# Moving two copies of the scan layer's ScalarE order, and leaving one background place empty

## The chip, the cores and the metric

The kernel runs on one core of one Trainium2 chip. The metric is the device time of one execution in microseconds. Before the change it is 13172.89 us, the median of 3 runs (13163.58 to 13174.3).

## The reference

The program is a chain of four layers on `x` of 8 x 64 x 64 x 64, all in fp32. Only layer 0 is touched. It normalises the 64 channels, projects them to two halves of 128, convolves one half (3 x 3, depthwise, SiLU), and runs a selective scan over the 4096 pixels in four directions `k`, with 16 states `N` for each of 128 channels:

```
def step(h, inp):
    u_t, dt_t, B_t, C_t = inp
    h = h * jnp.exp(dt_t[..., None] * A) + dt_t[..., None] * B_t[:, :, None, :] * u_t[..., None]
    return (h, jnp.einsum('bkcn,bkn->bkc', h, C_t))
```

The four directions' results are summed, normalised, multiplied by SiLU of the other half (the gate `z`), projected back to 64 channels and added to `x`. A second block of the layer and three attention or normalisation layers follow; nothing of them changes here.

## The kernel before

`scan_layer` works image by image (8), and in each image through 16 **steps**: directions in the order 0, 2, 1, 3, and in each four chunks of 1024 pixels. A step has 16 **turns** `n`, counted from 0, one for each state. The order of all instructions is written out by hand (`manual_schedule`), and each engine runs its own in that order.

In turn `n` SP issues two loads of rows broadcast to 128 partitions, `bt` of three turns ahead (four buffers) and `ct` of one turn ahead (five buffers). ACT computes `decay` (L575), `a = exp(dt * A)`, two turns ahead. `unit` makes `bdu = bt * du` on DVE (L594, in PSUM), scans (L598, result `h`, three buffers), lets ACT copy the last column to `state` (L602), and lets POOL multiply `ct` by `h` (L607). PE adds that product into `yps` by a matmul with the identity (`sum_up`, L636), two turns late (`LAG`). In turns 3 and 8 (`BY_POOL`) the product with the step input is POOL's, in place in `bt` (L583), made two turns ahead; the scan then reads `bt`, and POOL's multiplication of the turn before is put off until after it.

At the ends of a step:

- the step input `dus = dt * u` is made on POOL for the next step (`step_input`, L548, after turn 11), and ACT copies it into PSUM as `du` (`place_input`, L554) in turn 15, when the last `bdu` has read the old one. There is one `du`.
- the sum of turn 15 is made by PE in turn 1 of the next step. `yps` has one buffer. `empty` (L616) lets ACT copy it to `y`, called at the head of `sum_up`, so in turn 2, behind that turn's `decay` and `state`; then PE opens the new `yps` with the old `y` or the skip term (L631) and adds turn 0.
- in the directions 1 and 3 ACT first gathers the chunk's columns into `ut` (L534).

Everything else is a queue of **background** items (`Background`). `before` takes one item at the head of a turn and issues its matmuls; `after`, at a turn's end, uses the item taken a turn earlier, mostly on ACT. Items of the next step (its projections, L487 to L525) go ahead of the others. Behind them wait, for the finished image, a normalisation and eight output projections (`xo`, L454, with a POOL multiplication of `z` and `y` each, L441); and for the next image, loads, a normalisation, eight projections into `pad`, eight gates (`z`, L390), and eight convolutions in four parts (`u`, L414). Gates and convolutions use SiLU, which costs ACT a table load, and another one for the next exponential. Ahead of step 15 of an image what is left in the queue is emptied at once.

Of the kernel before, what the change touches and what calls it, by code (L numbers as in the profile page):

```python
# [24 lines left out]
N = 16  # L25
# [139 lines left out]
class Background:  # L165
# [14 lines left out]
    def later(self, do):  # L180
        self.late.append(do)

    def before(self):
        self.now = None
        if self.queue:
            make, use = self.queue.popleft()
            self.now = (use, make() if make else None)

# [14 lines left out]
def scan_layer(cm, x_in, w, xh):  # L203

    tc, nc = cm.tc, cm.nc
    with ExitStack() as ctx:
# [51 lines left out]
        skip = cm.tile([DI, 1], "skip")  # L258
# [7 lines left out]
        bg = Background()  # L266
# [202 lines left out]
        def ordered(t, k, c):  # L469

            if k % 2 == 0:
                return t[:, bass.ts(c, CH)].rearrange("p (a b) -> p a b", b=S)
            q = CH // S
            return t.rearrange("p (h w) -> p w h", w=S)[:, c * q : (c + 1) * q, :]
# [70 lines left out]
        def step_input(ctl):  # L545

            ctl["dus"] = work.tile([DI, CH], F32, name="dus", tag="dus", bufs=1)
            nc.gpsimd.tensor_tensor(ctl["dus"], ctl["dt"], ctl["ut"]["u"], ALU.mult)  # L548

        def place_input(ctl):  # L550


            ctl["du"] = psy.tile([DI, CH], F32, name="du", tag="du")
            nc.scalar.copy(ctl["du"], ctl["dus"])  # L554
# [11 lines left out]
        def load(ctl, n, t):  # L566

            bcr = ctl["bc"].rearrange("(t n) l -> t n l", t=2)
            name = "bt" if t == 0 else "ct"
            ctl[name, n] = bcp.tile([DI, CH], F32, name=name, tag=name, bufs=4 + t)  # L570
            nc.sync.dma_start(ctl[name, n], bcr[t, n].unsqueeze(0).broadcast_to([DI, CH]))

        def decay(ctl, n):
            ctl["a", n] = work.tile([DI, CH], F32, name="a", tag="a", bufs=3)
            nc.scalar.activation(  # L575
                ctl["a", n], ctl["dt"], AF.Exp, scale=amat[:, ctl["k"], n : n + 1]
            )
# [7 lines left out]
        def unit(ctl, n, nxt):  # L585

            k, state = ctl["k"], ctl["state"]
            a, bt, ct = ctl.pop(("a", n)), ctl.pop(("bt", n)), ctl.pop(("ct", n))
            flip = slice(None, None, -1 if k >= 2 else 1)
            last = 0 if k >= 2 else CH - 1  # L590
            z = bt
            if n not in BY_POOL:
                z = psy.tile([DI, CH], F32, name="bdu", tag="bdu")
                nc.vector.tensor_tensor(z, bt, ctl["du"], ALU.mult)  # L594
            if n == N - 1 and nxt:
                place_input(nxt)
            h = work.tile([DI, CH], F32, name="h", tag="h", bufs=3)
            nc.vector.tensor_tensor_scan(  # L598
                h[:, flip], a[:, flip], z[:, flip],
                0.0 if state is None else state[:, n : n + 1], ALU.mult, ALU.add,  # L600
            )
            nc.scalar.copy(ctl["new"][:, n : n + 1], h[:, last : last + 1])  # L602
            ready.append((ctl, n, ct, h))
            if n + 1 not in BY_POOL:
                while ready:
                    ctl, n, ct, h = ready.pop()
                    nc.gpsimd.tensor_tensor(ct, ct, h, ALU.mult)  # L607
                    pending.append((ctl, n, ct))
# [3 lines left out]
        def empty():  # L612

            if full:
                ctl = full.pop()
                nc.scalar.copy(  # L616
                    ordered(ctl["y"], ctl["k"], ctl["c"]),
                    ctl["ps"].rearrange("p (a b) -> p a b", b=S),
                )

        def sum_up():


            empty()
            ctl, n, ct = pending.popleft()
            if n == 0:
                ctl["ps"] = psy.tile([DI, CH], F32, name="yps", tag="yps")
                wt, src = (skipd, ctl["u"]) if ctl["k"] == 0 else (cm.ident, ctl["y"])
                so, half = ordered(src, ctl["k"], ctl["c"]), BK // S
                for i in range(CH // BK):  # L630
                    nc.tensor.matmul(  # L631
                        ctl["ps"][:, bass.ts(i, BK)].rearrange("p (a b) -> p a b", b=S),
                        wt, so[:, i * half : (i + 1) * half, :], start=True, stop=False,
                    )
            for i in range(CH // BK):
                nc.tensor.matmul(  # L636
                    ctl["ps"][:, bass.ts(i, BK)], cm.ident, ct[:, bass.ts(i, BK)],
                    start=False, stop=(n == N - 1),
                )
            if n == N - 1:  # L640
                full.append(ctl)
# [7 lines left out]
        def prepare(b, s):  # L649

            if b not in images:
                return None
            u, zd, y = images[b]
            k, c, i = steps[s]
            dt, bc, ut, items, soft3 = project(u, k, c)
            if b == 0 and s < NCH:
                items = later.pop(s, []) + items
            bg.add(items, first=True)
            new = work.tile([DI, N], F32, name="state", tag="state", bufs=3)
            return dict(  # L660
                k=k, c=c, u=u, y=y, dt=dt, bc=bc, ut=ut, soft3=soft3, new=new, state=None,
                first=(i == 0),
            )
# [5 lines left out]
        def start(b):  # L669
            u, zd, items, gates, convs = before(b)  # L670
            y = io.tile([DI, L], F32, name="y", tag="y")
            images[b] = (u, zd, y)
            bg.add(items)
            if b == 0:
                for s in range(1, NCH):
                    later[s] = convs[2 * s] + convs[2 * s + 1]
                bg.add(convs[0] + convs[1])
                later[NCH] = gates
            else:
                bg.add(gates)  # L680
                for conv in convs:
                    bg.add(conv)


        with tc.manual_schedule():
            start(0)
            bg.drain()
            ctl = prepare(0, 0)
            bg.drain()
            ctl["soft3"]()  # L690
            for n in range(3):
                load(ctl, n, 0)
            load(ctl, 0, 1)
            for n in range(2):
                decay(ctl, n)
            step_input(ctl)
            place_input(ctl)
            for b in range(NB):
                for s in range(len(steps)):
                    if s + 1 < len(steps):  # L700
                        nxt = prepare(b, s + 1)
                    else:
                        while bg.queue:
                            bg.before()
                            bg.after()
                        nxt = prepare(b + 1, 0)

                    def ahead(do, m, *args):
                        if m < N:
                            do(ctl, m, *args)  # L710
                        elif nxt:
                            do(nxt, m - N, *args)

                    for n in range(N):
                        bg.before()
                        ahead(load, n + 3, 0)
                        ahead(load, n + 1, 1)
                        ahead(decay, n + 2)
                        ahead(product, n + 2)
                        unit(ctl, n, nxt)  # L720
                        if len(pending) + len(ready) > LAG:
                            sum_up()
                        bg.after()

                        if n == (13 if b == 0 and s < NCH else 8) and nxt:
                            nxt["soft3"]()
                        if n == (13 if b == 0 and s < NCH else 11) and nxt:
                            step_input(nxt)

                        if s == 0 and n == LAG + 2 and b > 0:  # L730
                            bg.add(after(b - 1, images[b - 1][2], images.pop(b - 1)[1]))
                        if s == (1 if b else NCH) and n == 0 and b + 1 < NB:
                            bg.add(later.pop(NCH, []))
                            start(b + 1)
                    if nxt:
                        if not nxt["first"]:
                            nxt["state"] = ctl["new"]
                    ctl = nxt
            while pending:
                sum_up()  # L740
            empty()
            bg.add(after(NB - 1, images[NB - 1][2], images[NB - 1][1]))
            bg.drain()
# [1137 lines left out]
```

## Time and profile before

| | us |
|---|---|
| median of 3 runs | 13172.89 |
| profiled execution, time | 13181.03 |
| profiled execution, span | 13179.2 |
| DVE busy | 10982.4 (83% of the span) |
| PE busy | 11127.1 (84%) |
| ACT busy | 7731.6 (59%) |
| POOL busy | 6776.3 (51%) |
| in the scans' stretch, 121 to 7724 us: DVE busy | 7163.89 of 7603 |
| POOL, PE, ACT busy there | 6050.95, 6061.36, 4793.03 |

The page is one execution taken by the hardware profiler. A group's row gives line, engine, operation, result and inputs, shape and count; then busy time and mean nanoseconds of one; then the engine's idle time just before the group's instructions and what ended it. In a timeline the columns are start, length, engine, line, operation, and in brackets the idle time before. A wait for several semaphores is put down to the one that came last.

### The profile page before, as it was taken

The page shows a single profiled execution, that of the slowest core. Times are in us where ns is not written, and L with a number is a line of the kernel's source. Part 1 is how long each engine was busy: PE and PEld are TensorE (multiplying, and loading weights), DVE is VectorE, ACT ScalarE, POOL GpSimd, SP SyncE. Part 2 cuts the span into 40 slices and gives each one's busy share as a digit, 9 for nine tenths or more (in the row PEclk, how much of TensorE's full clock was granted, in tenths as well). Part 3 has the DMA queues.
Part 4 walks back from the last instruction along what each step waited for, and adds up shares of the span by engine and source line. Part 5 has one row for each costly group of instructions (what it writes and reads, how often), then busy time and mean ns, then how long its engine had stood idle before and what let it go on. Part 6 is the DMA issues. An engine that isn't in the chain of part 4 may idle for free. (4 is left out here: it accounts for less than half of the span.)

```text
span 13179.2 us, 115966 instructions
## 1 busy us (share of the span) xinstructions
PE 11127.1 (84%) x36395; PEld 4134.4 (31%) x36395; DVE 10982.4 (83%) x7626; ACT 7731.6 (59%) x10048; POOL 6776.3 (51%) x3126
## 2 busy tenths in 40 slices
PE   8787887788888878877877779999997778999999
PEld 2232232232232232322322223323324554333332
DVE  6999999999999999999999958686686786666666
ACT  5675666665666766665765536455464674544544
POOL 5778878778778778778778840000002772000000
PEclk9898999898999999999998879999998788999999
DMA  5888888888888888888888840000001010000000
GB/s 196 289 281 291 302 290 294 293 286 301 292 285 306 288 291 300 290 285 303 288 287 299 289 158 9 23 13 17 17 6 63 29 37 25 5 17 17 5 11 6
DMA packets 684840, 2333.69 MB, mean 177 GB/s; under 512 B 96784, under 2 KB 97456, under 8 KB 681648
## 3 DMA queue, kind: packets, MB, share of 16 engines
q1 hardware_dynamic: 684208, 2326.13, 51.1%
q8 instruction: 290, 4.75, 0.1%
q14 instruction: 342, 2.80, 0.1%
HBM read 2240.69 MB, written 76.28 MB: 176 GB/s over the span
## 5 line engine op out<-in xcount | busy, mean ns | idle before, releaser
L607 POOL TENSOR_TENSOR ct<-ct,h 128x1024 f32<-128x1024 f32 x2048 | 4820.7, 2369 | 1546.7 <-DVE h L598 779.5
L636 PE MATMUL yps<-ct,ident 128*128 128x512 f32 x8192 | 4157.3, 641 | 542.2 <-POOL ct L607 540.9
L598 DVE TENSOR_TENSOR_SCAN h<-a,state,bdu 128x1024 f32<-128x1024 f32 x1344 | 3153.9, 2347 | 193.1 <-POOL ct L607 15.1
L892 DVE TENSOR_TENSOR sum<-sum,ex 128x1024 f32<-128x1024 f32 x1920 | 2348.0, 1223 | 767.0 <-ACT ex L885 653.6
L885 ACT ACTIVATE ex<-sc 128x1024 f32<-128x1024 f32 x2048 | 1985.1, 1021 | 1526.5 <-PE sc L880 1526.3
L636 PEld LDWEIGHTS yps<-ct,ident 128*128 128x128 f32 x8192 | 1573.6, 202 | 3084.1 <-issue 1893.4
L575 ACT ACTIVATE a<-dt,amat 128x1024 f32<-128x1024 f32 x2048 | 2337.2, 1142 | 22.7 <-POOL dt L528 19.5
L594 DVE TENSOR_TENSOR bdu<-bt,du 128x1024 f32<-128x1024 f32 x1792 | 2194.4, 1225 | 186.7 <-ACT du L554 123.8
L899 PE MATMUL av<-ex,v 128*64 128x512 f32 x8192 | 1985.9, 606 | 0.0
L602 ACT COPY state<-h 128x1 f32<-128x1 f32 x2048 | 381.4, 186 | 2251.4 <-DVE h L598 2247.6
L880 PE MATMUL sc<-q,k 16*128 16x512 f32 (+1 forms) x8192 | 1655.0, 628 | 5.0 <-ACT ex L885 4.4
L598 DVE TENSOR_TENSOR_SCAN h<-a,bdu 128x1024 f32<-128x1024 f32 x448 | 1024.5, 2287 | 65.7 <-ACT state L602 4.8
L899 PEld LDWEIGHTS av<-ex,v 128*64 128x64 f32 x8192 | 497.7, 136 | 1361.6 <-issue 1358.2
L880 PEld LDWEIGHTS sc<-q,k 16*128 16x128 f32 (+1 forms) x8192 | 562.5, 184 | 1078.4 <-ACT ex L885 744.3
L1197 POOL TENSOR_TENSOR gt<-gt,pad 128x1024 f32<-128x1024 f32 x16 | 34.9, 2181 | 1617.6 <-ACT gt L1196 1535.5
L631 PE MATMUL yps<-y,ident 128*128 128x512 f32 x384 | 344.7, 1039 | 386.3 <-ACT y L616 386.3
L583 POOL TENSOR_TENSOR bt<-bt,dus 128x1024 f32<-128x1024 f32 x256 | 603.1, 2356 | 5.2 <-DMA bt<-bc 4.7
L598 DVE TENSOR_TENSOR_SCAN h<-a,state,bt 128x1024 f32<-128x1024 f32 x192 | 566.3, 2950 | 20.5 <-POOL bt L583 19.0
L405 PE MATMUL vps<-pad,convd 128*128 128x512 f32 x1152 | 535.4, 594 | 1.5 <-ACT z L390 1.5
L1570 DVE RECIPROCAL r<-e 128x512 f32<-128x512 f32 x128 | 420.7, 3323 | 0.0
L512 ACT ACTIVATE dt<-tps,dtb 128x512 f32<-128x512 f32 x256 | 175.1, 684 | 361.6 <-PE tps L505 361.6
L528 POOL TENSOR_TENSOR dt<-dt,e 128x1024 f32<-128x1024 f32 x128 | 300.9, 2351 | 111.0 <-ACT dt L525 111.0
(402 smaller groups left out, 10439.3 us busy)
## 6 DMA issues: line engine op xcount, KB each, us to landing
bt<-bc SPq DMA_DIRECT2D x2048, 512.0 KB
ct<-bc SPq DMA_DIRECT2D x2048, 512.0 KB
x<-x SPq DMA_DIRECT2D x12, 2048.0 KB
bc<-e SPq DMA_DIRECT2D x256, 64.0 KB
zd<-z SPq DMA_DIRECT2D x64, 256.0 KB
z<-zd SPq DMA_DIRECT2D x64, 256.0 KB
x<-x SPq DMA_DIRECT2D x32, 512.0 KB
part<-x SPq DMA_DIRECT2D x128, 128.0 KB
```

The costliest lines, as they stand in the source:

```text
L405: nc.tensor.matmul(held[0].rearrange("p (r c) -> p r c", c=S), convd[:, t, :], pad[:, j * rows + dy : (j + 1) * rows + dy, dx : dx + S], s ...
L575: nc.scalar.activation(ctl["a", n], ctl["dt"], AF.Exp, scale=amat[:, ctl["k"], n : n + 1])
L583: nc.gpsimd.tensor_tensor(bt, bt, ctl["dus"], ALU.mult)
L594: nc.vector.tensor_tensor(z, bt, ctl["du"], ALU.mult)
L598: nc.vector.tensor_tensor_scan(h[:, flip], a[:, flip], z[:, flip], 0.0 if state is None else state[:, n : n + 1], ALU.mult, ALU.add,)
L607: nc.gpsimd.tensor_tensor(ct, ct, h, ALU.mult)
L636: nc.tensor.matmul(ctl["ps"][:, bass.ts(i, BK)], cm.ident, ct[:, bass.ts(i, BK)], start=False, stop=(n == N - 1),)
L880: nc.tensor.matmul(sc[:, e, :], k[r : r + d, bass.ts(j, 128)], qs[i][r : r + d, :], start=True, stop=True,)
L885: nc.scalar.activation(ex, sc, AF.Exp)
L892: nc.vector.tensor_tensor(sums[i], sums[i], ex, ALU.add)
L899: nc.tensor.matmul(avs[i][r, :], v[:, j, r], ex[:, e, :], start=(j == 0), stop=(j == TQ - 1))
L1570: nc.vector.reciprocal(r[n][s], e[n][:, s])
```

## The change

Three things in the order of instructions; no operation is added or taken away.

1. `empty` is called at the head of every turn and no longer in `sum_up`. The copy of `y` is thus ACT's first work of turn 2, ahead of that turn's `decay`.
2. In turn 13, the fourteenth, no background item is taken. Its use would have followed turn 14.
3. In turn 15 the `decay` of the next step's turn 1 is issued after `unit`, so that the copy to `du` and the `state` of turn 15 stand ahead of it.

```
-    def before(self):
+    def before(self, skip=False):
         self.now = None
-        if self.queue:
+        if self.queue and not skip:
...
         def sum_up():
-            empty()
             ctl, n, ct = pending.popleft()
...
                     for n in range(N):
-                        bg.before()
+                        empty()
+
+                        bg.before(n == N - 3)
                         ahead(load, n + 3, 0)
                         ahead(load, n + 1, 1)
-                        ahead(decay, n + 2)
+                        if n < N - 1:
+                            ahead(decay, n + 2)
                         ahead(product, n + 2)
                         unit(ctl, n, nxt)
+                        if n == N - 1:
+                            ahead(decay, n + 2)
                         if len(pending) + len(ready) > LAG:
                             sum_up()
                         bg.after()
```

## The prediction

> **What bounds the kernel now.** I read the share in 40 slices first, then the costliest groups, then who waited for whom on DVE, then two stretches of the timeline. From the page (groups: busy us, mean ns of one, then idle time before and what ended it):
>
> ```profile
> DVE  6999999999999999999999958686686786666666
> ...
> L607 POOL TENSOR_TENSOR ct<-ct,h 128x1024 f32<-128x1024 f32 x2048 | 4820.7, 2369 | 1546.7 <-DVE h L598 779.5
> ...
> L598 DVE TENSOR_TENSOR_SCAN h<-a,state,bdu 128x1024 f32<-128x1024 f32 x1344 | 3153.9, 2347 | 193.1 <-POOL ct L607 15.1
> ...
> L598 DVE TENSOR_TENSOR_SCAN h<-a,state,bt 128x1024 f32<-128x1024 f32 x192 | 566.3, 2950 | 20.5 <-POOL bt L583 19.0
> ```
>
> DVE fills the scan layer (its scans run from 123 to 7723 us); every microsecond saved or lost there counts fully, one on ACT, PE or POOL only if DVE feels it. An ordinary turn lasts 3.7 us on DVE: L594 1.23, scan 2.29 or 2.35, small gaps. The fourth row is the same scan with its input `bt` in SBUF, made by POOL (turns 3 and 8): 2.95 us mean, though its shortest is 2.32; the 64 without a state take 3.11 against 2.27. So 192 x 0.63 + 64 x 0.84 = 174 us are lost inside these scans. Turn by turn in the trace: 154 at turn 8, 20 at turn 3.
>
> DVE's waits between 500 and 7600 us begin with:
>
> ```profile
> DVE bdu L594 <- ACT du L554: 64.6, 18, 7.6
> DVE h L598 <- POOL bt L583: 37.3, 37, 1.9
> DVE h L598 <- POOL ct L607: 16.3, 19, 1.1
> ```
>
> For the whole layer, without the start, the `du` wait is 75.7 us, and two more of 5.1 and 4.2 us at the same place are put down to a DMA: **85 us**. By cause: 3.5 in the first image (turns where POOL's `dus` is late), 7.6 and 7.6 there and 6 x 5.1 in images 1 to 6 behind gates (`z`), 24.4 behind `xo`, 11.4 behind a convolution's `u`. Here is a gate case on ACT (start us, us):
>
> ```profile
> 4519.91 0.18 ACT L602 COPY state<-h 128x1 f32<-128x1 f32 x1
> 4520.11 1.28 ACT L390 ACT_TABLE_LOAD   x1
> 4521.40 0.69 ACT L390 ACTIVATE z<-zps,inb 128x512 f32<-128x512 f32 x1
> 4522.11 1.28 ACT L575 ACT_TABLE_LOAD   x1
> 4523.40 1.15 ACT L575 ACTIVATE a<-dt,amat 128x1024 f32<-128x1024 f32 x1
> 4524.46 1.00 ACT L554 COPY du<-dus 128x1024 f32<-128x1024 f32 x1
> ```
>
> Between the state of turn 14 and `du` stand a background item and an exponential, 4.35 us; DVE waits 5.09 for this `du`. Each gate turn costs ACT 4.54 us against DVE's 3.74, so ACT was late already.
>
> The second stretch is one step's turns 2 to 8:
>
> ```profile
> 3351.03 1.01 ACT L616 COPY y<-yps 128x1024 f32<-128x1024 f32 x1
> ...
> 3355.66 2.81 PE L636 MATMUL yps<-ct,ident 128*128 128x512 f32 x4
> ...
> 3358.50 0.32 SPq L571 DMA_DIRECT2D ct<-bc  x1
> ...
> 3362.45 2.37 POOL L607 TENSOR_TENSOR ct<-ct,h 128x1024 f32<-128x1024 f32 x1 [2.20 <-DMA ct<-bc]
> ...
> 3367.89 3.71 DVE L598 TENSOR_TENSOR_SCAN h<-a,state,bt 128x1024 f32<-128x1024 f32 x1
> ```
>
> `y` is copied out, PE may reuse `yps` and sums turn 0, that frees one of five `ct` buffers, SP loads turn 5's `ct` into it, POOL gets it 3.95 us later and 2.2 late, and its product of turn 6 (3367.09 to 3369.44) runs into the scan of turn 8, which takes 3.71 instead of 2.33. On average `ct` of turn 5 starts 2.1 us after its scan. The scans of step 4 of three images, where it was on time, have POOL done 0.14 us ahead and lose nothing: the rest of the order fits.
>
> **What the Trainium skill says.** "SBUF — State Buffer", Who interferes with whom: VectorE and GpSimd share one port pair as an exclusive lock, which an operation with two SBUF inputs needs. The trace agrees: `bt` scans last up to 4.47 us beside POOL, scans of `bdu` (PSUM) stay within 2.346 to 2.350. "Trainium Architecture — The Big Picture", Inside one NeuronCore: each engine has its own instruction stream and they meet only in semaphores. It agrees: `du` stands behind work it does not need. "ScalarE: Activation LUTs", What ACT_TABLE_LOAD costs: 1283 ns and a drain of 1380. The load is 1.28 here; no drain shows, work goes on within 0.03 us.
>
> **The change part by part.** No operation is added or removed. I laid out ACT's new order from the code and priced it with the rows above; zero is the end of the scan of turn 15.
>
> *du first, nothing in the fourteenth turn.* The item left out of turn 13 would have run after the state of turn 14. So that state is followed by `du`, and the exponential goes behind the state of turn 15. The 4.35 us are gone. Moreover every item comes about one turn later per step, so gates fall before turn 15 only in step 10 (three of them, 2.4 us of lateness; `du` is there in time), `xo` in step 4, turns 7 to 12, and `u` at other turns. What stays: 3.5 (POOL sets it) and 7.6 - 4.35 = 3.3. **Gain 85 - 6.8 = 78.** The moved exponential ends at 1.35 and is wanted by the scan of turn 1 at about 5: covered.
>
> *y first.* The copy moves ahead of an exponential (1.14) and of the wait for turn 2's scan: from 3351.03 to 3347.8 in the step shown, 3.2 earlier. Its input, the sum of turn 15, ends at 6.3 us (median) and is not what it waits for; ready is at 7.5 to 8.3 instead of 11.4. `ct` of turn 5 then lands before it is wanted wherever it was under 3 us late. POOL's chain without a wait ends 0.15 us ahead of the scan of turn 8. The exponential behind it (turn 4's) ends by 10.5 and is wanted at 14.8: covered.
>
> That holds in steps 0 to 10 and 14. In images that prepare a next one, steps 11 to 15 now begin with convolution or gate work on ACT just after turn 15: 1.35 + 1.97 (load, Silu) + 1.92 (`ut`) + 2.43 (load, exponential) and turn 1's work put `y` at 9.3 in steps 12 to 14, at 12.5 in step 11 (two gates), at 11.1 in step 15. With lateness now of 3.2, 4.5, 4.1, 2.8, 2.0 us in steps 11 to 15, 3.9, 2.4, 2.0, 0.7, 1.7 remain; a scan loses about lateness less 0.5, at most 2.13 (1.95 late cost 1.40, 0.94 cost 0.41): 2.1 and 1 of waiting, 1.9, 1.5, 0.2, 1.2. In step 4 a gate product on POOL (1.27) now stands just before turn 8's scan: 1.1. Together 9.0 x 7 images + 1.1 = 64 of the 154. **Gain 90.** The wait for POOL's `bt` (37.3) falls in the same proportion: **20**. At turn 3, half of the 20, as the `xo` products leave the step's end: **10**.
>
> *What it costs.* In step 11 the exponential of turn 3 ends at 12.3 and is wanted at 11.2: 7 x 1.1 = **8**. Two buffers' worth of slack cover the others. Fifteen places per step instead of sixteen leave three convolution parts (five in the first image) to be emptied at the head of step 15, at once on PE: three parts of two taps, 12 matmuls; 12 of L636 in a row take 5.31 us in the timeline. PE has no consumer due before 7.5 us; not in the trace, so bounded from 0 to 5 us each; I take **5** in all. SP's loads keep their order and are issued earlier; a stretch with more of them at once is not in the trace, and I give it nothing, with 0 to 30 us in the range.
>
> Sum: 78 + 90 + 20 + 10 - 8 - 5 = 185. The profiled execution took 13181.0 (span 13179.2, 1.8 around it), 8.1 above the median 13172.9. So 12996 on its footing, **12988 as a median**.
>
> **The rivals.** *Only du heals (0.14).* If `ct` of turn 5 was held by DMA rather than by its free buffer, the scans of turn 8 still lose 154. For: DMA is busy 0.84 of the layer, 3.95 us from issue to use. Against: its issue follows turn 0's sum by 0.03 us. Then -78 + 13 to at best -110: 13063 to 13108. *All heals (0.06):* late steps too, -185 - 60: 12928. *y blocks ACT (0.05), the slower side.* ACT runs in order; the copy now stands in front of turn 4's exponential, so if PE's sum of turn 15 came late, exponentials and then scans would. It decides from a copy start of 14.8 - 1.14 - 1.4 = 12.3 us; to lose 26 us net it must reach about 14 at all 127 boundaries (1.7 us each, 211 in all). Then 13200. Against: 6.3 median, 12.0 at the ninetieth per cent, and those are boundaries where `du` or `xo` was late. *It does nothing (0.03):* DVE's saved time reappears as waits for POOL (6051 busy of 7603): 13173. Each step holds 18 products of 2.36 and two more, 47 us of 59.
>
> **How the numbers follow.** My own case has 0.72 and, with its bounds (lateness in the late steps, bursts, loads), 12945 to 13040. With the smaller gains the range is 12930 to 13105. Chances, by 0.2% (26 us), about what a measurement of this kernel can tell from no change: faster 0.91, same 0.04, slower 0.05.
>
> **What would show it.** Right: DVE's wait for `du` near 7 us outside the start; the `bt` scans' mean down to 2.6 or less; POOL's wait for `ct<-bc` (556 us) under half; late scans of turn 8 in steps 11 to 13 and 15 only. Wrong: an ACT idle before L616 of some 2 us or more each time, waits on `a` over 20 us, or turn 8 unchanged though `y` is early.

## The result, and the profile after

The kernel after takes 12999.92 us (median of 4 runs, 12995.89 to 13005.02) against 13173.59 for the kernel before: ratio 0.9869, 95% interval 0.9852 to 0.9886. That is 174 us less; 12988 had been forecast. The profiled execution's span went from 13179.2 to 12998.2, 181.0 less (the profiled execution of before was 7 us above its median, which is why the traces differ by more than the medians), and all of it lies in the scan layer: from the first scan to the end of the last, 7599.9 us became 7418.3, and the rest of the span stayed at 5579 to 5580.

The page after, the rows that answer to those shown of before, and one more of each (L594):

```profile
DVE  6999999999999999999999948677686786766766
...
L607 POOL TENSOR_TENSOR ct<-ct,h 128x1024 f32<-128x1024 f32 x2048 | 4807.8, 2362 | 1377.0 <-DVE h L598 814.0
...
L598 DVE TENSOR_TENSOR_SCAN h<-a,state,bdu 128x1024 f32<-128x1024 f32 x1344 | 3153.6, 2346 | 196.5 <-POOL ct L607 10.0
...
L594 DVE TENSOR_TENSOR bdu<-bt,du 128x1024 f32<-128x1024 f32 x1792 | 2194.9, 1225 | 109.9 <-ACT du L554 54.9
...
L598 DVE TENSOR_TENSOR_SCAN h<-a,state,bt 128x1024 f32<-128x1024 f32 x192 | 508.0, 2646 | 17.0 <-ACT state L602 9.0
```

The row of L594 in the page before:

```profile
L594 DVE TENSOR_TENSOR bdu<-bt,du 128x1024 f32<-128x1024 f32 x1792 | 2194.4, 1225 | 186.7 <-ACT du L554 123.8
```

Two rows carry the gain. The scans of `bt` last 2.65 us on average where they had lasted 2.95, although nobody touched them; the scans of `bdu` did not move by more than a nanosecond. The wait for `du` is 54.9 us, of which 48.2 lie ahead of the very first `bdu`, as before (48.1 of 123.8); 6.7 are left of 85. DVE's waits in the steady stretch, 500 to 7500 us (us in total, times, longest):

```profile
DVE h L598 <- POOL ct L607: 10.8, 12, 1.6
DVE h L598 <- ACT state L602: 10.7, 10, 2.3
DVE h L598 <- POOL bt L583: 8.8, 14, 1.9
DVE h L598 <- DVE bdu L594: 8.7, 18, 0.5
DVE h L598 <- ACT a L575: 5.4, 8, 2.0
```

`du` is gone from the list, POOL's `bt` fell from 37.3 to 8.8, and two lines that stand for late exponentials (`a` itself, and ACT's `state` as the instruction that came last) grew: together from 9.9 to 20.9 over the layer.

The timeline shows the chain of the prediction in the same step of the same image (step 6 of image 3), whose scan of turn 8 now starts 72.7 us earlier on the clock:

```profile
3276.26 1.01 ACT L616 COPY y<-yps 128x1024 f32<-128x1024 f32 x1 [1.11 <-PE yps L635]
...
3279.15 1.88 PE L635 MATMUL yps<-ct,ident 128*128 128x512 f32 x4
...
3281.06 0.89 SPq L571 DMA_DIRECT2D ct<-bc  x1
...
3287.91 2.37 POOL L607 TENSOR_TENSOR ct<-ct,h 128x1024 f32<-128x1024 f32 x1 [0.35 <-DVE h L598]
3290.24 2.37 POOL L583 TENSOR_TENSOR bt<-bt,dus 128x1024 f32<-128x1024 f32 x1
...
3292.55 2.37 POOL L607 TENSOR_TENSOR ct<-ct,h 128x1024 f32<-128x1024 f32 x1
...
3295.18 2.33 DVE L598 TENSOR_TENSOR_SCAN h<-a,state,bt 128x1024 f32<-128x1024 f32 x1
```

The copy of `y` starts 9.3 us after the end of the step before, where it had started at 11.4. POOL now waits for the scan and no longer for the load (0.35 <-DVE in place of 2.20 <-DMA), its product of turn 6 ends at 3294.92, and the scan of turn 8 starts 0.26 us later and takes 2.33 us instead of 3.71.

### The profile page after: what moved, and what is told of

Its sections match the earlier page's. It is cut to its first block, busy times and chain, and to the rows that moved or that the text cites. A ratio compares the mean times of both kernels' runs of the same rounds, so it can differ in the third digit from the quotient of the medians.

```text
span 12998.2 us, 115945 instructions
## 1 busy us (share of the span) xinstructions
PE 11180.4 (86%) x36395; PEld 4120.7 (32%) x36395; DVE 10894.5 (84%) x7626; ACT 7732.2 (59%) x10048; POOL 6768.3 (52%) x3126
## 5 line engine op out<-in xcount | busy, mean ns | idle before, releaser
L635 PE MATMUL yps<-ct,ident 128*128 128x512 f32 x8192 | 4218.1, 649 | 534.7 <-POOL ct L607 533.5
L594 DVE TENSOR_TENSOR bdu<-bt,du 128x1024 f32<-128x1024 f32 x1792 | 2194.9, 1225 | 109.9 <-ACT du L554 54.9
L598 DVE TENSOR_TENSOR_SCAN h<-a,state,bt 128x1024 f32<-128x1024 f32 x192 | 508.0, 2646 | 17.0 <-ACT state L602 9.0
L487 PE MATMUL dps<-ut,wx 128*32 128x512 f32 x256 | 167.6, 743 | 246.1 <-ACT ut L534 157.9
L630 PE MATMUL yps<-y,ident 128*128 128x512 f32 x384 | 302.3, 918 | 72.3 <-ACT y L616 71.4
```

Source lines behind the costliest of these rows:

```text
L598: nc.vector.tensor_tensor_scan(h[:, flip], a[:, flip], z[:, flip], 0.0 if state is None else state[:, n : n + 1], ALU.mult, ALU.add,)
L635: nc.tensor.matmul(ctl["ps"][:, bass.ts(i, BK)], cm.ident, ct[:, bass.ts(i, BK)], start=False, stop=(n == N - 1),)
```

## The experiments

All compare with the kernel before on the same chip (medians of it between 13166 and 13184). "Loss at turn 8" and "at turn 3" is the time of those scans above 2.32 us (2.27 for those without a `state`), the shortest of the kernel before, summed over 128 steps; "`du`" is DVE's wait for it without the start. The intervals reach 12 to 22 us to each side, so the times alone do not settle a difference of some 20 us between two rows of different groups; the three right columns are read from the traces.

| kernel | ratio (95% interval) | us against before | loss at turn 8 | at turn 3 | `du` |
|---|---|---|---|---|---|
| before | 1 | 0 | 152 | 22 | 85 |
| after | 0.9869 (0.9852 to 0.9886) | -174 | 65 | 26 | 7 |
| y alone | 0.9886 (0.9869 to 0.9902) | -151 | 33 | 21 | 80 |
| empty place and du | 0.9950 (0.9933 to 0.9966) | -65 | 134 | 26 | 7 |
| empty place alone | 0.9958 (0.9941 to 0.9974) | -58 | 164 | 22 | 13 |
| du alone | 0.9989 (0.9980 to 0.9998) | -14 | 159 | 26 | 42 |
| before, six ct buffers | 0.9867 (0.9850 to 0.9883) | -179 | 11 | 20 | 75 |
| after, six ct buffers | 0.9833 (0.9816 to 0.9849) | -221 | 26 | 13 | 7 |
| after, no SiLU in turns 12 to 15 | 0.9934 (0.9918 to 0.9951) | -94 | 50 | 38 | 3 |
| the same, six ct buffers | 0.9894 (0.9877 to 0.9910) | -147 | 16 | 36 | 3 |
| after, no SiLU in turn 14 | 0.9825 (0.9811 to 0.9838) | -234 | 18 | 32 | 10 |
| the same, six ct buffers | 0.9810 (0.9796 to 0.9823) | -251 | 11 | 22 | 10 |

### One part at a time

y alone:

```
                     for n in range(N):
+                        empty()
                         bg.before()
...
         def sum_up():
-            empty()
```

> The kernel before with the copy of y alone moved to the head of a turn; du and the background as before. Theory (free ct buffer, then port): the scans' loss at turn 8 falls from 154 us to under 50, DVE's wait for du stays near 85, and the background items of a step's start stay where they were, so fewer boundaries find ACT late than in the kernel after: 13173 - 150 = 13023, 12995 to 13055. Rival, that the gain is mostly du and the empty place: under 60 us gained, 13115 or more. Rival, that y in front of an exponential blocks ACT: waits of DVE on a of over 20 us and no gain.

Measured 13015.13, 151 less. The loss at turn 8 fell to 33 us, the wait for `du` stayed, and DVE's waits for exponentials are 9 us, so the rival in which `y` blocks ACT is not met here. The copy of `y` starts 8.1 us after the step's end (median) where it started at 11.4.

The empty place and du, y as before (`bg.before(n == N - 3)`, and the `decay` of turn 15 behind `unit`):

> The kernel before with the empty fourteenth place and du ahead of the exponential, y where it was. Theory: the wait for du falls from 85 to 7 us, the loss at turn 8 stays between 130 and 175, so 13173 - 78 = 13095, 13080 to 13115. If the two gains overlap (items moved behind the boundary make y late), this one and y alone add up to more than the 174 gained together, by some 50. Rival, that the background's place feeds the late ct buffers: the loss at turn 8 falls too, below 100 us, and the time is under 13060.

Measured 13101.95, 65 less, with the loss at turn 8 at 134. The rival in which the background's place feeds the `ct` buffers falls. y alone and this one make 216 together, 42 more than the change. The traces show 32 of it: 65 us are lost at turn 8 in the kernel after, 33 with y alone. The overlap had been forecast, its cause only in part, as the last group shows.

Then each half of the second by itself:

> The kernel before with the fourteenth place left empty, and nothing else. Theory: at the step's end ACT saves the background item but keeps the exponential in front of du (1.15 us); the waits behind xo and u go, the gate boundaries keep about 1 us each (7) and 4.4 in the first image: DVE's wait for du falls from 85 to about 15. y stays late, the scans' loss at turn 8 stays at 130 or more. 13170 - 60 = 13110, 13090 to 13130. Rival, that du's place in front of the exponential is the main thing: under 25 us gained.

> The kernel before with du ahead of the exponential, and nothing else. Theory: where a gate or a convolution stands before it, du saves a table load and an exponential (2.43 us), behind xo 1.14: the wait for du falls from 85 to about 46. 13170 - 39 = 13131, 13115 to 13150. Rival, that the empty place does nothing more: the same as both together, 13102.

The empty place alone brought 58 us, and 60 had been expected; the wait for `du` fell to 13. du alone brought 14 (its interval reaches from 3 to 26), and 39 had been expected. Its wait did fall, from 85 to 42, but the time went elsewhere. DVE's waits in that kernel, 130 to 7720 us:

```profile
DVE h L598 <- POOL bt L583: 53.6, 44, 3.6
DVE bdu L594 <- ACT du L554: 41.8, 19, 5.2
DVE h L598 <- ACT state L602: 19.0, 17, 2.2
```

Of the 43 us saved, 16 came back as waits for POOL's `bt` (37.3 before), 14 behind ACT's `state` (5.4 before), and 11 as longer scans of `bt` (152 + 22 to 159 + 26). A likely reason, which no run tests by itself, is that the stall at the step's end had also been the time in which POOL and ACT caught up. Of the 78 us of `du` in the kernel after, the empty place carries 72 (85 to 13 when alone), since with it the item itself is gone from there, and not only its order.

### Is it the buffer?

Six `ct` buffers, nothing of the change (room came from putting the residual's tiles `xr` into the unused half of `xn`):

```
-            ctl[name, n] = bcp.tile([DI, CH], F32, name=name, tag=name, bufs=4 + t)
+            ctl[name, n] = bcp.tile([DI, CH], F32, name=name, tag=name, bufs=4 + 2 * t)
...
-            xn = io.tile([C, L], F32, name="xn", tag="xn", bufs=1)
+            xn = xnr[:C]
...
-                xr = work.tile([C, BK], F32, name="xr", tag="xr", bufs=3)
+                xr = xnr[C:, bass.ts(j % 3, BK)]
```

> The kernel before with six ct buffers in place of five; nothing of the change. (Room: the residual's tiles xr lie in the unused half of xn.) Theory: the load of turn 5's ct no longer waits for the sum of turn 0, so the loss at turn 8 falls from 154 us to under 40 with y still copied 11.4 us after the boundary; 13173 - 150 = 13023, 12995 to 13055. Rival, that DMA is late by itself (busy 0.84): the loss stays over 120 us and the time within 30 us of 13173. Rival, that y's early copy helps PE or ACT in another way than by the buffer: the same, no gain here.

Measured 12987.15: -179 with `y` still copied at 11.4 us and `du` still late. That is faster than the range expected: with `ct` in time DVE's waits for POOL's `bt` and `ct` fell too, from 54.5 to 11.8 us, which the expectation had left out. From its page:

```profile
L599 DVE TENSOR_TENSOR_SCAN h<-a,state,bt 128x1024 f32<-128x1024 f32 x192 | 459.8, 2395 | 0.5 <-POOL bt L584 0.5
```

2.40 us a scan, 0.5 us of waiting for POOL where it was 19.0. This settles the mechanism: the copy of `y` as such did not make `ct` late, and neither did the length of the load, but the buffer that PE freed behind that copy. In the kernel before POOL waited for turn 5's `ct` in 107 of 128 steps; the load was issued 0.03 us after PE's sum of turn 0, only 1.9 us ahead of its need, and took 4.0 us to POOL's start (medians). With six buffers it is issued 4.5 us ahead of that sum and 6.7 ahead of the need. One more buffer does what the early copy does, in nearly all steps (step 10 keeps 1.1 us).

> The kernel after with six ct buffers (room as in the other). Theory: the 68 us that the scans of turn 8 still lose there, in steps 11 to 15, are the same buffer wait; they fall under 20 and the time to 13000 - 55 = 12945, 12925 to 12965. Rival, that those late steps are late by PE's or ACT's load at the boundary and not by the buffer: within 15 us of 13000.

Measured 12945.16. The forecast 12945 was met, though 26 us are left at turn 8 where under 20 had been said, most of it in steps 11 (1.5 us each) and 15 (1.4), where ACT reaches `y` only 12 to 13 us after the step's end.

### Why steps 11 to 15 stay late

The first idea was ACT: SiLU items with their table loads just after the step's end. Their place was moved, by a mark on gates and convolutions, and the rest of the queue was left for step 15:

```
+    def before(self, skip=False, light=False):
         self.now = None
+        if light and self.queue and getattr(self.queue[0][1], "heavy", False):
+            skip = True
         if self.queue and not skip:
...
-                        while bg.queue:
-                            bg.before()
-                            bg.after()
...
-                        bg.before(n == N - 3)
+                        bg.before(n == N - 3, n > N - 5)
```

> The kernel after, with no SiLU item taken in turns 12 to 15 (so none of its table loads stands between turn 13 and the copy of y), and with what is left over of the queue not emptied ahead of step 15 but used in the places after it. Theory: the late steps 11 to 15 are late by that ACT work; the loss at turn 8 falls from 65 us to under 20, DVE's waits on a and on ACT's state from 16 to about 5. 13000 - 60 = 12940, 12915 to 12970. Rival, that PE's convolution matmuls make them late: under 15 us gained, since the matmuls stay in the same steps.

> The same with six ct buffers. Theory: what six buffers left at turn 8 in steps 11 and 15 (20 us) and the waits on a (26) go too: 12945 - 33 = 12912, 12890 to 12930. Rival, that the two cure the same loss only: within 10 us of 12940.

Both missed, and on the slower side: 13090.28 and 13037.07, 80 and 75 us more than the forms without this edit, at -174 and -221. The items were where they should be, but two more convolutions now reached into step 0 of the next image, the products of the `xo` items lay across the end of step 4, and `y` was copied 12 to 14 us after the ends that open steps 15 and 0, with ACT itself idle there. The timeline of one of these kernels (no SiLU in turns 12 to 15, five buffers; step 15 of image 2) shows why:

```profile
2889.17 1.85 PE L491 MATMUL dps<-u,wx 128*32 128x512 f32 x2 [4.81 <-ACT e L499]
2890.95 2.83 PE L639 MATMUL yps<-ct,ident 128*128 128x512 f32 x4
2893.81 1.92 ACT L620 COPY y<-yps 128x1024 f32<-128x1024 f32 x1 [4.70 <-PE yps L639]
```

PE stands 4.81 us in front of the second projection of the next step until ACT has emptied the first one; the sum of turn 15, which `y` waits for, stands behind it, and ACT is idle 4.70 us. Two `mm` banks (buffers in PSUM) serve all background work; a convolution takes one from its first part to its use, three items later. When it is open across a step's end, the two projections have a single bank between them. The kernel after has the same in its late steps. In step 12 of image 2 `y` was already copied by 2698.04:

```profile
2694.10 1.98 PE L635 MATMUL yps<-ct,ident 128*128 128x512 f32 x4
...
2696.12 1.92 ACT L616 COPY y<-yps 128x1024 f32<-128x1024 f32 x1 [0.42 <-PE yps L635]
...
2699.58 1.91 PE L487 MATMUL dps<-ut,wx 128*32 128x512 f32 x2 [3.50 <-ACT e L495]
2701.43 3.79 PE L630 MATMUL yps<-y,ident 128*128 128x512 f32 x4
```

So it is not `y` that is late in steps 12 to 14, but PE: it stands there 3.2 to 3.6 us a step on average in the kernel after. y alone agrees: in its step 12 the copy starts at 7.6 us, PE stands 4.1, and 1.8 are still lost at turn 8.

The last pair tests that: SiLU items are refused in turn 14 alone (`n == N - 2`), and what is left of the queue is again used in step 15's places. By the order written out, no convolution should then hold a bank across both projections of the next step.

> The kernel after, with no SiLU item taken in turn 14 and the leftover of the queue used in step 15's free places; by the order written out, every convolution now ends before the next step's projections begin, so none holds one of PE's two mm banks across a step's end. y stays as early as in the kernel after (8.4 to 9 us). Theory (bank): the trace of the kernel after shows PE idle 3.5 us ahead of its second projection in step 12, waiting for ACT to empty the one free bank, with y already copied; without an open convolution the loss at turn 8 in steps 11 to 15 falls from 8.1 to under 2 us an image, 65 to under 25 in all; against the kernel before -174 - 55 = -229, -200 to -250. Rival (ACT's lateness alone): y is no earlier, so steps 12 to 14 keep over 1 us each and the gain over the kernel after is under 25.

> The same with six ct buffers. Theory: little of the buffer's wait is left for the sixth to cure; the loss at turn 8 falls under 10 us, the loss at turn 3 and the waits on a stay; against the kernel before -240, -225 to -265. Rival: bank and buffer are separate losses, and this one gains over 25 us on the one with five.

Measured 12946.60 (-234) and 12929.59 (-251). With five buffers `y` is copied at 8.7 us in steps 12 to 14, exactly as in the kernel after, yet the loss at turn 8 there fell from 1.79, 1.73 and 1.14 us a step to 0.11, 0.00 and 0.03. The same step as above:

```profile
2672.07 1.04 PE L491 MATMUL dps<-ut,wx 128*32 128x512 f32 x2
...
2672.76 1.92 ACT L620 COPY y<-yps 128x1024 f32<-128x1024 f32 x1
...
2674.73 3.68 PE L634 MATMUL yps<-y,ident 128*128 128x512 f32 x4 [1.61 <-ACT y L620]
```

The second projection no longer waits, and PE now waits for `y`, as it should. The convolutions do not all end before the first projection, as had been expected; but in steps 12 to 15 of this image the SiLU that frees their bank is over 6.0 to 6.3 us after the step's end, and the second projection starts at 6.0 to 8.1, where in steps 12 to 14 of the kernel after it starts at 12.1 to 12.7. PE's waits for the first projection to be emptied, 83 us in the kernel after, are gone from the whole trace; 34 us of waiting for that SiLU came in their place. The bank theory holds, its rival falls. The sixth buffer adds 17 us more (on the same chip, and the five runs of each kernel do not overlap), within the first theory's range in time, with 11 us left at turn 8 where under 10 was said; its rival, over 25, is not met. 12929.59 is the fastest kernel of the study, 0.9810 of the one before.

## Why the prediction was right

Step by step, the sum's terms against what DVE's records show (us saved, before less after):

| term | forecast | measured |
|---|---|---|
| wait for `du` | 78 | 78 (85 to 7) |
| scans of turn 8 | 90 | 86 (152 to 65) |
| wait for POOL's `bt` | 20 | 29 (37.3 to 8.8, whole layer) |
| scans of turn 3 | 10 | -4 (22 to 26) |
| waits for exponentials | -8 | -11 (9.9 to 20.9) |
| queue emptied ahead of step 15 | -5 | about -4, all in the first image, and contained in the row above |
| wait of scans for POOL's `ct` | none | 6 (17.2 to 11.1) |
| sum | 185 | 184; the layer became 181.6 shorter |

That the two sums agree to 1 us is in part luck: five terms are off by 3 to 14 us, and these cancel. The prediction split the 174 us lost in scans into 154 and 20; summed scan by scan they are 152 and 22.

**What held.** The bound (DVE), the port between DVE and POOL as the place where a late `ct` turns into DVE time, and the free buffer as the reason for the late `ct`. The port is what the Trainium skill, "SBUF — State Buffer", Who interferes with whom, says of an operation with two SBUF inputs; here it shows in the six-buffer kernel, whose scans of `bt` shrink to 2.40 us with the same operands, while those that read PSUM stay at 2.35. POOL's wait for `ct<-bc` fell from 556 to 330 us; the forecast had said under half, so it fell less. At turn 5, the one that the argument is about, it fell from 256 to 81.

**What was mis-sized.** *Turn 3.* The step of the sum that failed is "half of the 20, as the `xo` products leave the step's end". POOL's eight products of an image lay between turn 11 of step 3 and turn 2 of step 4; four stay there, and four went to turns 7 to 12 of step 4, beside POOL's two operations for the next step. In the trace POOL's products then start 3 to 4 us late in turns 0 and 1 of step 5, where they had been 2 to 3 late. In front of these turns POOL waits for `ct<-bc`, and with the sixth buffer they are 1.1 and 2.0 us late and the loss at turn 3 is 13 us in place of 26: here too a buffer that came free late takes part. The loss of steps 4 and 5 moved by one step and stayed (22 to 21 us), and 5 us came new in step 12.

*The late steps.* Steps 11 to 15 were forecast to keep 2.1, 1.9, 1.5, 0.2 and 1.2 us at turn 8 and kept 1.75, 1.79, 1.73, 1.14 and 1.67. The total was close, 6.9 against 8.1 an image, but the reason held only in steps 11 and 15; for steps 12 to 14 the agreement is luck. The loss had been put down to ACT's table loads in front of `y`. `y` came when forecast (8.7 in steps 12 to 14 where 9.3 was said, 12.1 in step 11, 11.6 in step 15), but in steps 12 to 14 the loss was that of the bank. The prediction had evidence in its own figures: the lateness of 4.5 and 4.1 us in steps 12 and 13 of the kernel before is larger than in the other steps, and in that trace PE stands 5.1 and 6.2 us a step at the same place. Step 13 was also misread: the copy was taken to start at 11.4 us there, as elsewhere, and the trace has 13.2; from 13.2 to 9.3 the same reckoning would have left 0.2 us of lateness and not 2.0.

*The emptied queue.* The 5 us were about right as a sum, but they lie in one place. In images 1 to 6 step 15 took 58.7 us, before 58.6. In the first image it took 63.1, before 59.3: PE had a run of convolution matmuls that ended 10.6 us after the step's end, the sum of turn 15 stood behind it, `y` was copied at 16.4, and DVE waited 4.3 us for exponentials.

**The rivals.** "Only du heals" falls by the six buffers. "y blocks ACT" did not decide, but its mechanism exists: ACT was idle 70 us in front of L616 (7.7 before), 0.5 us a step, where the prediction had named 2 us as the sign of being wrong. Its other sign, waits on `a` over 20 us, was just reached if ACT's `state` is counted in (20.9, but 9.9 before), and not by `a` alone (5.4). With SiLU kept out of turns 12 to 15 and five buffers, DVE waited 24 us for `a` in steps 15 and 0. The copy starts there at 13.0 and 13.8 us (medians), past the 12.3 that the prediction gave as the point of decision.

## What to carry to other kernels

When one engine is the bound, follow each of its overlong instructions back through the other engines to the first buffer that is not free; the cure may be the order on an engine that is idle a third of the time, or one more buffer, and the two can be told apart by trying the buffer alone. A bank that is held from the first part of a work item to its last is a resource of the schedule like any engine: see to it that no such item is open where several other items need the rest of the pool. A stall that is removed need not pay in full (du alone took 43 us of waiting away and gained 14), so look at what is late next before adding two gains.

## What the runs showed of the hardware

A scan of `bt` and a GpSimd product that meet do not share time: the one that starts first keeps its length, and the other grows. Of the 256 scans of `bt` in the kernel before, 110 started with more than 0.2 us of a POOL product still to run; each grew by what was left of that product, less 0.11 to 0.18 us (by 1.38 us where 1.55 were left in the step shown of before, by 2.1 where nearly all was, up to 4.47 us in all). In 14 others the scan started first and kept its length, and POOL's product, begun 0.08 to 0.55 us later, grew in its turn by what was left of the scan, less 0.20 to 0.22, to 3.9 to 4.4 us in place of 2.36. The remaining scans met no product and lost at most 0.03 us. Both outcomes stand side by side in step 12 of the kernel before, in images 5 and 6:

```profile
5625.98 2.36 POOL L607 TENSOR_TENSOR ct<-ct,h 128x1024 f32<-128x1024 f32 x1
5626.04 4.45 DVE L598 TENSOR_TENSOR_SCAN h<-a,bt 128x1024 f32<-128x1024 f32 x1 [1.82 <-POOL bt L583]
...
6578.20 2.29 DVE L598 TENSOR_TENSOR_SCAN h<-a,bt 128x1024 f32<-128x1024 f32 x1 [1.68 <-POOL bt L583]
6578.75 3.89 POOL L607 TENSOR_TENSOR ct<-ct,h 128x1024 f32<-128x1024 f32 x1 [0.59 <-DMA ct<-bc]
```

In the first, POOL's next product had nothing to wait for and started 0.06 us ahead of the scan. In the second its `ct` landed 0.59 us later, so the scan was first. On DVE the price does not show as a wait: it lies inside the length of the scan.

For the `mm` banks, the Trainium skill, "Perfetto Trace Analysis", Matmuls, advises to rotate independent groups through different banks so that emptying one overlaps the next. The runs put a price on the case in which a group that is held open leaves one bank to rotate in: PE idle 3.50 and 4.81 us in the two steps shown, and 1.1 to 1.8 us of DVE time a step in steps 12 to 14 of the kernel after.
